# A four-layer network on one Trainium2 core: second expert choices of layer 0 in slots of their own, and layer 1's constant tiles written by POOL

## The chip, the cores and the metric

The kernel runs on one core of a Trainium2 chip. That core has five engines with an instruction queue each: PE (TensorE, matrix products), DVE (VectorE), ACT (ScalarE), POOL (GpSimd) and SP (SyncE, which here only issues DMAs). Each queue runs its instructions in order; semaphores make an instruction wait for another engine or for a DMA. The metric is the device time of one execution in microseconds (us).

## The reference, cut to what matters

Four layers stand one after another. Each takes a layer norm of x (4 sequences of 512 tokens of 128 numbers) and adds an attention part and a feed-forward part to it:

```
xn = layernorm(x)
x = x + L0_attn(xn) + L0_ffn(xn)     # ... the same for L1, L2, L3
```

Layer 0's attention has a window of 64 keys. The feed-forward parts of layers 0 and 1 are mixtures of 8 experts: every token goes to the two experts of highest probability, and the result is the sum of both outputs times their gates.

```
top_w, top_idx = top_k(softmax(h @ router.T), 2)
y = sum over the two: gate * expert(h)
```

## The kernel before

**Stages.** `run` (L1716) traces `setup`, `l0`, `l1_zeros`, `l0_ffn`, `l1_attn`, `l1_ffn`, `l2_attn`, `l3`. A scheduler orders each engine's queue from its own estimate of readiness. Inside a block marked `manual_schedule` the instructions of PE, DVE, ACT and POOL keep the order in which they were written, but instructions from outside the block may be put between them when the scheduler believes them ready.

**Layer 0's attention** (`l0`) loops over 32 half-tiles n (16 tiles of 128 tokens, 8 heads each) and five steps of run-out. One step makes scores (PE, L355 and L361), row maxima (DVE, L372 and L373), exponentials (ACT, L384), then turned weights, weighed values (L411, L413, L414) and projections (L430, L431) of the steps before. Four times in a step, at `pull()`, a piece of other work is put into the queues: up to a generator's next `yield`. That other work is, in order, the layer norms, the small attention of the feed-forward part (`mix`), and `route`.

**Routing** (`route`, L1170) finds for each token its two experts and their ranks by comparing all pairs of 8 probabilities (1024 numbers a partition: L1180, L1183, L1184, L1187, L1191), and a place for each (token, choice) in a list of slots that is sorted by expert. Then it sends rows of tokens to their slots in DRAM by 32 indirect DMAs from POOL (L1250), each of 128 rows: 16 tiles by two choices, all into one tensor `slots`. The framework sees two writes of one tensor as dependent, so each of them waits until the one before has landed.

**The expert stage** (`on_slots`, L664) reads the slots in 10 groups of four tiles: SP loads a group (L679, three buffers), PE turns it (L682), ACT copies it, DVE copies the expert's weights (L650), PE multiplies (L656, L688), DVE copies the result out (L693), SP stores it (L694). POOL gathers the results by the same indices (L1260).

**Constants of layer 1** (`l1_zeros`, L949): six tiles for layer 1's attention (kn, qn0, qn1, vv0 to vv2) are zeroed on DVE (L959), and columns of ones are put in (L963, L964, L967). They lie in a pool at the right end of SBUF, where the pools of layer 0 have been; the first of them waits for what used that memory last, among it `rows`, from which the 32 indirect DMAs read.

`setup` also fills `slots` with zeros (L91), so that rows that no token takes hold numbers.

Of the kernel before, what the change touches and what calls it, by code (L numbers as in the profile page):

```python
# [9 lines left out]
F32 = mybir.dt.float32  # L10
# [3 lines left out]
ALU = mybir.AluOpType  # L14
# [3 lines left out]
P = 128  # L18
B, T, D = 4, 512, 128
# [7 lines left out]
SLOT_TILES = (2 * NTOK + E * (P - 1)) // P  # L27


def bc(ap, axis, n):  # L30

    a = ap.unsqueeze(axis)
    shape = list(a.shape)
    shape[axis] = n
    return a.to_broadcast(shape)


class Net:
# [5 lines left out]
    def setup(self):  # L44
        self.routed, self.sending = {}, False

        self.sides = []
        nc, tc, ctx, io = self.nc, self.tc, self.ctx, self.io
        self.const = const = ctx.enter_context(tc.tile_pool(name="const", bufs=1))
        self.keep = keep = ctx.enter_context(tc.tile_pool(name="keep", bufs=1))  # L50
        self.work = ctx.enter_context(tc.tile_pool(name="work", bufs=2))

        self.x = keep.tile([P, NT, D], F32, tag="x", name="x")
        self.xn = keep.tile([P, NT, D], F32, tag="xn", name="xn")

        self.xnT_wide = keep.tile([P, 64 + NTOK], F32, tag="xnT", name="xnT")
        self.xnT = self.xnT_wide[:, 64:]
        nc.gpsimd.memset(self.xnT_wide[:, 0:64], 0.0)
        xin = io["x"].rearrange("(t p) d -> p t d", p=P)
        for b in range(B):  # L60
            nc.sync.dma_start(self.x[:, b * TPB : (b + 1) * TPB, :], xin[:, b * TPB : (b + 1) * TPB, :])

        self.w = {}

        self.first_stack = ExitStack()
        self.first = self.first_stack.enter_context(tc.tile_pool(name="first", bufs=1))
        self.load("l0_", nc.sync)
        self.load("l0f_", nc.sync)

        self.ident = const.tile([P, P], F32, tag="ident", name="ident")  # L70
        make_identity(nc, self.ident)
        self.identb = const.tile([P, P], BF16, tag="identb", name="identb")
        nc.vector.tensor_copy(self.identb, self.ident)
        self.ones = const.tile([P, P], F32, tag="ones", name="ones")
        nc.gpsimd.memset(self.ones, 1.0)

        with tc.tile_pool(name="masks", bufs=1) as tmp:
            self.masks(tmp)


        self.before = const.tile([P, P], F32, tag="before", name="before")
        nc.gpsimd.affine_select(self.before, self.ones, [[1, P]], ALU.is_gt, 0.0, base=0, channel_multiplier=-1)
        self.tile_no = const.tile([1, SLOT_TILES, E], F32, tag="tile_no", name="tile_no")
        nc.gpsimd.iota(self.tile_no, [[1, SLOT_TILES], [0, E]], base=0, channel_multiplier=0, allow_small_or_imprecise_dtypes=True)

        dram = ctx.enter_context(tc.tile_pool(name="rows", bufs=1, space=bass.MemoryType.DRAM))
        self.slots = dram.tile([SLOT_TILES * P, D], F32, tag="slots", name="slots")
        self.results = dram.tile([SLOT_TILES * P, D], F32, tag="results", name="results")
        empty = const.tile([P, D], F32, tag="empty", name="empty")
        nc.gpsimd.memset(empty, 0.0)  # L90
        nc.sync.dma_start(self.slots.rearrange("(t p) d -> p t d", p=P), bc(empty, 1, SLOT_TILES))  # L91

        self.parts0 = keep.tile([P, TPB, 2, D], F32, tag="parts0", name="parts0")


        self.bd = const.tile([P, P], F32, tag="bd", name="bd")
        nc.gpsimd.affine_select(self.bd, self.ones, [[-8, 16], [0, 8]], ALU.is_ge, 0.0, base=0, channel_multiplier=1)
        nc.gpsimd.affine_select(self.bd, self.bd, [[8, 16], [0, 8]], ALU.is_ge, 0.0, base=7, channel_multiplier=-1)

        self.low = const.tile([P, E, E], F32, tag="low", name="low")  # L100
        nc.gpsimd.affine_select(
            self.low, self.ones[:, 0 : E * E].rearrange("p (e f) -> p e f", f=E), [[1, E], [-1, E]], ALU.is_gt, 0.0,
            base=0, channel_multiplier=0,
        )
# [559 lines left out]
    def on_slots(self, layer, sb, ps1, tokens, hidden, w2):  # L664


        nc = self.nc
        expert = self.routed[layer][2]
        slots = self.slots.rearrange("(t p) d -> p t d", p=P)
        results = self.results.rearrange("(t p) d -> p t d", p=P)  # L670
        GROUP = 4
        for t0 in range(0, SLOT_TILES, GROUP):
            n = min(GROUP, SLOT_TILES - t0)
            _, es = nc.values_load_multi_w_load_instructions(
                expert[0:1, t0 : t0 + n], engines={mybir.EngineType.PE, mybir.EngineType.DVE}, min_val=0, max_val=E - 1,
                skip_runtime_bounds_check_because="a count of experts, at least 0, and no more than 7 by a minimum",
            )
            xs = sb.tile([P, GROUP, D], F32, tag="xs", name="xs")
            nc.sync.dma_start(xs[:, 0:n, :], slots[:, t0 : t0 + n, :])  # L679
            pt = ps1.tile([P, GROUP, P], F32, tag="xs", name="xs_ps")  # L680
            for i in range(n):
                nc.tensor.transpose(pt[:, i, :], xs[:, i, :], self.ident)  # L682
            xT = sb.tile([P, GROUP, P], F32, tag="xT", name="xT")
            tokens(xT[:, 0:n, :], pt[:, 0:n, :])
            y_ps = ps1.tile([P, GROUP, D], F32, tag="y", name="y_ps")
            for i, parts in hidden(xT, es):
                for c, h in enumerate(parts):
                    nc.tensor.matmul(  # L688
                        y_ps[:, i, :], h, w2[:, bass.ds(es[i], 1), c, :].rearrange("p a d -> p (a d)"), start=(c == 0),
                        stop=(c == len(parts) - 1),  # L690
                    )
            y = sb.tile([P, GROUP, D], F32, tag="ys", name="ys")
            nc.vector.tensor_copy(y[:, 0:n, :], y_ps[:, 0:n, :])  # L693
            nc.sync.dma_start(results[:, t0 : t0 + n, :], y[:, 0:n, :])  # L694
# [254 lines left out]
    def l1_zeros(self):  # L949

        nc = self.nc
        self.zero_stack = ExitStack()
        sb = self.zero_stack.enter_context(self.tc.tile_pool(name="z1", bufs=1, side="right"))

        qn = [sb.tile([P, 2, TPB, 16, 32], BF16, tag=f"qn{i}", name=f"qn{i}") for i in range(2)]
        kn = sb.tile([P, 2, TPB, 4, 32], BF16, tag="kn", name="kn")
        vv = [sb.tile([P, 2, TPB, 4, 32], F32, tag=f"vv{i}", name=f"vv{i}") for i in range(3)]
        for t in [kn] + qn + vv:
            nc.vector.memset(t, 0.0)  # L959

        for t in qn:
            for c in range(3):
                nc.vector.memset(t[32 * c : 32 * c + 32, :, :, :, 26 + c : 27 + c], 1.0)  # L963
        nc.vector.memset(kn[:, :, :, :, 24:26], 1.0)  # L964
        for t in vv:
            for hf in range(2):
                nc.vector.memset(t[:, hf, :, :, 16 * hf + 4 : 16 * hf + 5], 1.0)  # L967
        self.l1_tiles = qn, kn, vv

    def l1_attn(self):  # L970
# [199 lines left out]
    def route(self, layer, sb, bank, pr, rows):  # L1170


        nc, keep = self.nc, self.keep
        self.softmax8(sb, pr)
        a = sb.tile([P, NT, E, E], BF16, tag="t2_a", name="t2_a", bufs=1)
        c = sb.tile([P, NT, E, E], BF16, tag="t2_c", name="t2_c", bufs=1)
# [4 lines left out]
        if layer == "l0":  # L1181
            yield
        near.tensor_tensor(a, a, bc(self.low, 1, NT), ALU.mult)  # L1183
        nc.vector.tensor_tensor(c, other, own, ALU.is_gt)  # L1184
        if layer == "l0":
            yield
        near.tensor_tensor(a, a, c, ALU.add)  # L1187
        for _ in range(0 if layer == "l0" else 3):
            yield
        rank = sb.tile([P, NT, E], F32, tag="r_rank", name="r_rank", bufs=1)  # L1190
        nc.vector.tensor_reduce(rank, a, AX.X, ALU.add)  # L1191
        sel = sb.tile([P, NT, E], F32, tag="r_sel", name="r_sel", bufs=1)
        nc.vector.tensor_scalar(sel, rank, 1.5, None, ALU.is_lt)
        yield

        ct = bank()[:, 0 : 2 * NT * E].rearrange("p (k t e) -> p k t e", k=2, t=NT)
        nc.tensor.matmul(ct[:, 0, :, :], self.before, sel, start=True, stop=True)
# [36 lines left out]
        index = keep.tile([P, 2, NT], I32, tag=layer + "r_ix", name="r_ix", bufs=1)  # L1234
# [9 lines left out]
        for tt in range(NT):  # L1244
            for k in range(2):
                if layer == "l0" or tt < 6 or k == 0:
                    yield
                if layer == "l0" and k and tt % 4 == 3:
                    yield
                nc.gpsimd.indirect_dma_start(  # L1250
                    self.slots[:, :], bass.IndirectOffsetOnAxis(ap=index[:, k, tt : tt + 1], axis=0), rows[:, tt, :], None
                )
        self.routed[layer] = index, gate, expert

# [568 lines left out]
```

## Time and profile before

| | |
|---|---|
| median of 9 runs | 1299.41 us (1296.92 to 1305.3) |
| the profiled execution | 1307.66 us, of which the span of its instructions is 1305.8 us |
| PE busy | 1047.2 us, 80% of the span |
| DVE, ACT, POOL busy | 806.8, 730.4 and 446.4 us |
| mean granted PE clock | 0.878 of full speed |
| DMA | 35.35 MB, mean 27 GB/s |

The stages by their first and last instructions in the trace: layer 0's attention from the start to 348.6 us; its expert stage to 401.7 us; layer 1's attention to about 787 us; layer 1's experts to about 892 us; layers 2 and 3 to the end. A duration is printed per instruction, or in total when several alike are merged (x8). In square brackets stands how long the engine sat idle before, and what ended that. A wait is listed as "engine, line <- what it waited for: us in total, times, longest".

### The profile page before, as it was taken

How to read it: one execution, taken by the hardware profiler on the slowest of the kernel's cores; microseconds unless marked ns; L12 is line 12 of the kernel's file. 1: busy time of each engine (PE TensorE's matmuls, PEld its weight loads, DVE VectorE, ACT ScalarE, POOL GpSimd, SP SyncE). 2: the span in 40 equal slices, each digit the busy share in tenths (PEclk: the TensorE clock that was granted, in tenths of full speed). 3: DMA queues.
4: the chain of work that ended last, by engine and by line, in shares of the span. 5: the costliest groups of instructions: out<-in, count | busy, mean ns of one | idle time of the engine just before them, and what ended most of it. 6: DMA issues, size and time to landing. Idle time of an engine off the chain costs nothing.

```text
span 1305.8 us, 27780 instructions
## 1 busy us (share of the span) xinstructions
PE 1047.2 (80%) x11397; PEld 657.1 (50%) x11428; DVE 806.8 (62%) x1842; ACT 730.4 (56%) x1301; POOL 446.4 (34%) x579
## 2 busy tenths in 40 slices
PE   5897897994783587888888877993678988999887
PEld 3575676773682244455544447992323333434254
DVE  5485877762533765888788833553557867767343
ACT  4675675783431246677575662221457767876732
POOL 4554652333002554371333321003371542622200
PEclk9799999997896567989888987996579989999899
DMA  7000000000134200000000001211000000000001
GB/s 232 1 2 1 1 2 2 16 26 28 49 88 145 105 15 4 12 8 3 2 3 26 26 18 51 64 31 35 13 15 3 16 3 1 1 1 1 1 1 33
DMA packets 38891, 35.35 MB, mean 27 GB/s; under 512 B 4653, under 2 KB 35694, under 8 KB 38254
## 3 DMA queue, kind: packets, MB, share of 16 engines
q1 hardware_dynamic: 34670, 25.18, 6.1%
q0 software_dynamic: 4096, 8.40, 2.1%
q8 instruction: 91, 1.49, 0.4%
q14 instruction: 34, 0.28, 0.1%
HBM read 20.65 MB, written 12.91 MB: 26 GB/s over the span
## 4 chain that ended last, share of the span: by engine, by line
PE 32%; DVE 14%; ACT 10%; POOL 6%; issue 4%; DMA 1%; another core or an unknown queue 0%; ACTq 0%; POOLq 0%; DVEq 0%
PE o_ps L827 5%; ACT p L818 5%; PE sq_ps L748 5%; DVE max L782 5%; PE gu L1333 4%; DVE negm L786 3%; PE y_ps L688 2%; PE sk_ps L748 2%; PE qs_ps L802 1%; PE po L942 1%; POOL xn L206 1%; PE po L1671 1%; PE tr L232 1%; POOL parts L1260 1%; PE piece L1435 1%
## 5 line engine op out<-in xcount | busy, mean ns | idle before, releaser
L818 ACT ACTIVATE p<-sk_ps 128x1024 f32<-128x1024 f32 x288 | 279.9, 1028 | 103.4 <-PE sk_ps L748 48.4
L782 DVE TENSOR_REDUCE max<-sq_ps 128x4 f32<-128x512 f32 x320 | 203.9, 685 | 68.3 <-PE sq_ps L748 39.7
L786 DVE TENSOR_REDUCE negm<-sq_ps 128x1 f32<-128x512 f32 x256 | 163.4, 684 | 67.6 <-PE sq_ps L748 65.3
L748 PE MATMUL sq_ps<-kb,qb 64*128 64x512 bf16 (+3 forms) x640 | 138.1, 348 | 43.2 <-DVE negm L786 13.4
L827 PE MATMUL o_ps<-p,vv 128*32 128x128 f32 (+3 forms) x2304 | 171.4, 416 | 1.1 <-issue 0.7
L748 PEld LDWEIGHTS <-qb 32*128 32x128 bf16 (+1 forms) x1152 | 50.4, 96 | 170.9 <-issue 151.7
L1260 POOL DMA_INDIRECT parts<-results,r_ix x64 | 63.4, 991 | 199.2 <-DMA results<-ys 103.1
L384 ACT ACTIVATE p<-s_ps,nm,rs 128x128 f32<-128x128 f32 x256 | 93.2, 485 | 27.3 <-DVE nm L373 27.3
L827 PEld LDWEIGHTS o_ps<-p,vv 128*32 128x32 f32 x2304 | 61.3, 116 | 72.0 <-issue 63.9
L748 PE MATMUL sk_ps<-qs,kb 64*128 64x512 bf16 (+3 forms) x640 | 74.4, 340 | 10.3 <-ACT p L818 8.9
L804 ACT COPY qs<-qs_ps 128x1024 bf16<-128x1024 bf16 x32 | 32.4, 1012 | 65.4 <-PE qs_ps L802 65.4
L1333 PE MATMUL gu<-xT,gu 128*128 128x128 f32 x468 | 60.3, 284 | 1.5 <-ACT xT L1320 1.5
L1333 PEld LDWEIGHTS gu<-xT,gu 128*128 128x128 f32 x468 | 57.2, 199 | 2.1 <-ACT xT L1320 2.1
L372 DVE TENSOR_REDUCE nm<-s_ps 128x4 f32<-128x512 f32 x64 | 41.3, 684 | 23.7 <-PE s_ps L361 23.6
L1335 ACT ACTIVATE silu<-gu 128x384 f32<-128x384 f32 x39 | 19.1, 491 | 62.5 <-PE gu L1333 62.5
L361 PEld LDWEIGHTS s_ps<-kT,qT 64*64 64x64 f32 x1024 | 30.5, 143 | 41.2 <-issue 41.2
L1250 POOL DMA_INDIRECT slots<-rows,r_ix x32 | 31.2, 976 | 53.3 <-DMA slots<-rows,r_ix 52.4
L748 PE MATMUL sq_ps<-kd,qb 32*128 32x128 bf16 x512 | 35.8, 233 | 16.8 <-DVE max L782 14.8
L1250 POOL DMA_INDIRECT slots<-xn,r_ix x32 | 30.9, 965 | 53.6 <-DMA slots<-xn,r_ix 52.8
L324 POOL TENSOR_TENSOR sq<-q 128x1024 f32<-128x1024 f32 x12 | 22.8, 1904 | 61.6 <-ACT q L319 61.6
L1327 DVE COPY gu<-w_l1f_gu 128x704 f32 x39 | 20.4, 527 | 37.7 <-PE gu L1333 37.7
L232 PE MATMUL piece<-ident,xn 128*128 128x128 f32 x32 | 8.7, 371 | 41.2 <-DVE xn L206 39.6
(437 smaller groups left out, 2252.3 us busy)
## 6 DMA issues: line engine op xcount, KB each, us to landing
xs<-slots SPq DMA_DIRECT2D x18, 256.0 KB
results<-ys SPq DMA_DIRECT2D x18, 256.0 KB
w_l1f_gu<-in_l1f_gu SPq DMA_DIRECT2D x1, 2816.0 KB
slots<-empty SPq DMA_DIRECT2D x1, 2496.0 KB
w_l0f_w<-in_l0f_w SPq DMA_DIRECT2D x2, 1024.0 KB
w_l1f_down<-in_l1f_down SPq DMA_DIRECT2D x1, 1536.0 KB
x<-in_x SPq DMA_DIRECT2D x4, 256.0 KB
parts<-results,r_ix POOLq DMA_INDIRECT x64
```

The lines of the kernel that those rows point to most:

```text
L361: nc.tensor.matmul(ss[a][cols, k, :], qT[rows, 4 * u + k, cols], kT[rows, u, c0 : c0 + P], start=False, stop=(k == 3))
L372: nc.vector.tensor_reduce(nm[:, a, :], ss[a], AX.X, ALU.max, negate=True)
L384: nc.scalar.activation(p[:, a, k, :], ss[a][:, k, :], AF.Exp, bias=nm[:, a, k : k + 1], scale=rs[:, h : h + 1])
L748: nc.tensor.matmul(s[:, c : c + w], lhs(rows, which(hf, r), slice(i * P, i * P + P)), rhs(rows, which(hf, r), slice(o0, o0 + w)), start=(x ...
L782: nc.vector.tensor_reduce(places[step](maxima[n % 2][:, r, :, :]), s.rearrange("p (x c) -> p x c", c=P), AX.X, ALU.max)
L786: nc.vector.tensor_reduce(m[:, r, step : step + 1], s, AX.X, ALU.max, negate=True)
L804: nc.scalar.copy(qs, pt.rearrange("p x i c -> p x (i c)"))
L818: nc.scalar.activation(p, ks[pr], AF.Exp, scale=scale)
L827: nc.tensor.matmul(o[32 * r : 32 * r + 32, q0 : q0 + w], states[b]["v"](hf, j, g, r), p[r // 2][:, r % 2, c : c + w], start=(step == 0 and ...
L1250: nc.gpsimd.indirect_dma_start(self.slots[:, :], bass.IndirectOffsetOnAxis(ap=index[:, k, tt : tt + 1], axis=0), rows[:, tt, :], None)
L1260: self.nc.gpsimd.indirect_dma_start(parts[:, i, k, :], None, self.results[:, :], bass.IndirectOffsetOnAxis(ap=index[:, k, b * TPB + i : b ...
L1333: nc.tensor.matmul(gu[:, k, c, :], wgu[:, k, c * P : (c + 1) * P], xT[:, i, :], start=True, stop=True)
```

## The change

Three things are changed.

First, layer 0's second choices go to a DRAM tensor `slots2` of their own, also filled with zeros at the start. The two indirect DMAs of a tile no longer write the same tensor. The expert stage of layer 0 loads both tensors and DVE adds them (128 partitions by 512 numbers a group). Layer 1 goes on using `slots` alone.

Second, the memsets of `l1_zeros` are issued on POOL in place of DVE.

Third, the yields of `route` are moved in layer 0: the comparisons come one to a pull, three pulls more stand before the first indirect DMA, and the four additional pulls among the indirect DMAs are gone.

```
+        self.slots2 = dram.tile([SLOT_TILES * P, D], F32, tag="slots2", name="slots2")
...
-        nc.sync.dma_start(self.slots.rearrange("(t p) d -> p t d", p=P), bc(empty, 1, SLOT_TILES))
+        for t in (self.slots, self.slots2):
+            nc.sync.dma_start(t.rearrange("(t p) d -> p t d", p=P), bc(empty, 1, SLOT_TILES))
...
             nc.sync.dma_start(xs[:, 0:n, :], slots[:, t0 : t0 + n, :])
+            if layer == "l0":
+                xs2 = sb.tile([P, GROUP, D], F32, tag="xs2", name="xs2")
+                nc.sync.dma_start(xs2[:, 0:n, :], self.slots2.rearrange("(t p) d -> p t d", p=P)[:, t0 : t0 + n, :])
+                nc.vector.tensor_tensor(xs[:, 0:n, :], xs[:, 0:n, :], xs2[:, 0:n, :], ALU.add)
...
         for t in [kn] + qn + vv:
-            nc.vector.memset(t, 0.0)
+            nc.gpsimd.memset(t, 0.0)
...
-                nc.vector.memset(t[32 * c : 32 * c + 32, :, :, :, 26 + c : 27 + c], 1.0)
-        nc.vector.memset(kn[:, :, :, :, 24:26], 1.0)
+                nc.gpsimd.memset(t[32 * c : 32 * c + 32, :, :, :, 26 + c : 27 + c], 1.0)
+        nc.gpsimd.memset(kn[:, :, :, :, 24:26], 1.0)
...
-                nc.vector.memset(t[:, hf, :, :, 16 * hf + 4 : 16 * hf + 5], 1.0)
+                nc.gpsimd.memset(t[:, hf, :, :, 16 * hf + 4 : 16 * hf + 5], 1.0)
...
         near.tensor_tensor(a, a, bc(self.low, 1, NT), ALU.mult)
+        if layer == "l0":
+            yield
         nc.vector.tensor_tensor(c, other, own, ALU.is_gt)
...
-        for _ in range(0 if layer == "l0" else 3):
+        for _ in range(1 if layer == "l0" else 3):
             yield
...
-        yield
+        for _ in range(2 if layer == "l0" else 1):
+            yield
...
-                if layer == "l0" and k and tt % 4 == 3:
-                    yield
+                slots = self.slots2 if layer == "l0" and k else self.slots
                 nc.gpsimd.indirect_dma_start(
-                    self.slots[:, :], bass.IndirectOffsetOnAxis(ap=index[:, k, tt : tt + 1], axis=0), rows[:, tt, :], None
+                    slots[:, :], bass.IndirectOffsetOnAxis(ap=index[:, k, tt : tt + 1], axis=0), rows[:, tt, :], None
```

## The prediction

> **What bounds the kernel now.** The busy shares (PE 80%, DVE 62%) come first, but they are means over stages. The chain that ended last doesn't help here: the pieces that it lists begin at 412.9 us, and the change lies before that. So I read the waits between 300 and 349 us, the end of layer 0's attention, where the page's 40 slices show a dip:
>
> ```profile
> ACT p L384 <- DVE nm L373: 22.9, 2, 21.0
> PE s_ps L355 <- ACT p L384: 21.1, 1, 21.1
> DVE kn L959 <- DMA slots<-rows,r_ix: 20.6, 1, 20.6
> ```
>
> These are one wait seen three times. PE waits for ACT, ACT for DVE's small multiply L373, and L373 stands behind L959, the memset of kn, which waits for the indirect DMAs. VectorE's timeline shows the order of that queue:
>
> ```profile
> 304.77 1.41 DVE L372 TENSOR_REDUCE nm<-s_ps 128x4 f32<-128x512 f32 x2 [1.35 <-PE s_ps L361]
> 326.74 0.48 DVE L959 MEMSET kn<- 128x512 uint32 x1 [20.56 <-DMA slots<-rows,r_ix]
> 327.14 0.10 DVE L373 TENSOR_TENSOR nm<-nm,rs 128x8 f32<-128x8 f32 x1
> ```
>
> The memset was put between the last maxima but one and their scaling. The indirect DMAs run late: the 32 first issue at 241.6 us, the last at 324.2 us, one per 2.5 us, because each waits for the one before:
>
> ```profile
> L1250 POOL DMA_INDIRECT slots<-rows,r_ix x32 | 31.2, 976 | 53.3 <-DMA slots<-rows,r_ix 52.4
> ```
>
> Next the stretches (us; then busy PE, PEld, DVE, ACT, POOL; then granted clock, DMA share, GB/s):
>
> ```profile
> 255.00:298.00 43.00, 42.69 (x565) 33.05 (x570) 28.09 (x69) 37.18 (x103) 15.64 (x16) 1.00 0.08 25
> 305.00:327.00 22.00, 2.69 (x46) 2.38 (x46) 1.42 (x3) 0.58 (x1) 7.76 (x9) 0.64 0.08 28
> 327.00:335.00 8.00, 6.16 (x73) 4.97 (x72) 7.09 (x13) 3.96 (x10) 0.00 (x0) 0.50 0.00 0
> 349.00:402.00 53.00, 44.76 (x351) 41.85 (x351) 16.50 (x49) 21.31 (x32) 0.00 (x0) 0.97 0.32 94
> ```
>
> The undisturbed loop is bound by PE (42.69 of 43 us), 7.2 us a step (maxima at 254.84, 269.27, 283.67, 298.09, two steps apart); DVE has about 2.4 us a step free. After the stall the granted clock is 0.50 for 8 us. The expert stage is PE's too; DVE is busy for a third of it.
>
> **The stall and the run-out.** Idle gone: 20.6 us. Then I rebuild the run-out without memsets and with a warm clock. L373 comes at 306.2, where L372 ends. The exponentials of ACT (2.90) end at 309.2; the last scores start about 0.4 us before that, as the ones at 303.15 did, and take 0.65 + 1.10 us (1.10 at full clock, 1.99 after the stall); maxima 1.3, so the last exponentials start at 312.1 in place of 335.8: 23.7 us earlier. From there to the last DVE instruction of the stage the trace takes 12.8 us, with two memsets of vv and all the small ones between DVE's other work. With the durations of the rows (exponentials 2.9, turns 1.1, copies 0.7, weighing 1.15, DVE 1.2 under PE's projection 2.05, turns 1.1, copies 0.7, projection 2.05: 11.75 and a little for hand-overs) I get about 11.9, so 0.9 less. Sum: **−24.6 us**. Ends: −20.6 (the wait alone) to −28 (memset time, 8.1 us, all on the path).
>
> **What is late next.** The indirect DMAs must not be. Two of one tile now write different tensors, so only every second waits. POOL's rate without waits is that of the gathers, which read one tensor and don't depend on each other:
>
> ```profile
> 405.33 0.98 POOL L1260 DMA_INDIRECT parts<-results,r_ix  x1 [80.12 <-DMA w_l_lam<-in_l_lam]
> 406.62 0.95 POOL L1260 DMA_INDIRECT parts<-results,r_ix  x1 [0.31 <-issue]
> ```
>
> 1.26 us each, so a pair fits the 2.5 us of one landing, and 32 take 40 us. Three pulls more move the first from 241.6 to about 244 us; the last lands near 287, far before the run-out ends (about 322). If nothing overlaps, they take 82 us and end at 327.
>
> **Memsets on POOL.** They wait for the last landings, then run from about 287. POOL has nothing else until its gather (idle for 80.1 us before 405.33), so they cost nothing while they end before that. Time on POOL: vv 128x1024 f32 at 0.92 each (half of L1308's 1.80), kn and qn about 0.5 to 0.9 and 1.8 to 3.4 each (L1049 on POOL is listed as bf16, 315 ns for 256 numbers, L1387 214 ns for 128), and 13 small ones under 0.22: 9 to 13 us in all. Could they slow DVE, which is in the loop's slack then? One row says that the two engines can block each other:
>
> ```profile
> 238.74 1.97 POOL L324 TENSOR_TENSOR sq<-q 128x1024 f32<-128x1024 f32 x1 [23.99 <-ACT q L319]
> 239.31 1.54 DVE L1232 SCALAR_TENSOR_TENSOR r_sel<-r_rank,pr 128x128 f32<-128x128 f32 x1
> ```
>
> L1232 takes 0.28 elsewhere. Bounds: 0 to +13 us if every memset stopped DVE; I take 0, because DVE's rows in that stretch read PSUM (L372, L397, L414) and a memset reads nothing, unlike L324.
>
> [...]
>
> **Route, one pass a pull.** In steps 19 to 22 the maxima start at 214.24, 230.40, 242.27, 246.88, then 254.84: 40.6 us against 4 x 7.2, so 11.8 us over. In step 19 DVE has 4.8 us of its own and 10.7 of route (short waits within it counted), in step 20 4.8 and 7.4. Moved, about 6.1 of route (softmax 1.8, passes 1.23, 1.21, 1.22, 0.68) stay in step 19, about 6 come in step 20, 4.7 in step 21. DVE's excess over 7.2 a step falls from 8.3 + 5.0 to 3.7 + 3.6 + 2.3, so by 3.7 of 13.3. As the old order gives part of its excess back (step 21 took 4.6 us), I take **−2.5 us** (0 to −4).
>
> **The expert stage.** Added: 10 loads, 10 adds on DVE. SBUF adds of f32 in the trace: 128 numbers 0.29, 320 0.49, 640 0.83; so 512 take 0.69, in all 6.8 us. In the steady part the loads are there long before (issue at 372.66 and 373.67, turned at 382.0 and 392.4), and DVE is free for two thirds: 0. The start is different, since nothing can be loaded before layer 0's pools are free:
>
> ```profile
> SPq L679 <- DVE yT L424: 335.5, 1, 335.5
> ```
>
> SP issues at 348.41; PE turns the first group at 351.11 and the second at 352.53, having waited for DMAs both times. Both come before PE's first product in its queue, and so does now the fourth load, not the second. A load of 256 KB takes 0.83 us of all DMA engines (queue q1: 25.18 MB in 6.1% of the span) up to the 1.4 us seen between those two turns. Two loads more are 1.7 to 2.8, the add 0.7, a late third or fourth group up to 1: **+3 us** (1 to 7).
>
> **The second fill of zeros.** 2496 KB more at the start, issued last at 11.2 us; SP's next load is at 348.4 us. 8 us of DMA, 0 us (0 to 1).
>
> **Sum.** −24.6 − 2.5 + 3 = −24.1 us. The profiled execution (1307.66, span 1305.8) would become 1283.6. It stands 8 us above the median of the runs; the terms are absolute waits, so I take them from the median: 1299.41 − 24.1 = **1275.3 us**.
>
> **Rivals.**
> - The indirect DMAs still land one by one (a queue in order). They end at about 244 + 82.5 + 2 = 328, and the expert stage starts some 6 us later than forecast: 1281. For it: nothing in the trace has two indirect writes in flight. Against it: the gathers do overlap. Chance 0.12.
> - POOL's memsets stop DVE: up to 13 us given back, 1288. For it the 1.54 us row, against it what DVE reads there, and its slack. Chance 0.05.
> - More is won: all of the memset time (−28) and the route's −4, the start +1: 1268. For it: the first products run at clock 0.50 until 335 and some half-microsecond hand-overs went with the memsets. Chance 0.13.
> - Slower: DVE's queue is in order, and an add stands ahead of weight copies (L650) of the group that PE works on. If the scheduler puts the adds so early that each waits for its load, each of ten groups pays issue to landing (2.7), the second issue (0.4) and the add (0.7): 38 us against the 27.1 won, so 1310. It decides from 2.7 us a group on. Against it: three buffers, and loads in the trace that land 8 us ahead. Chance 0.04.
> - The change doesn't do what it says: another instruction that waits for the indirect DMAs or for the loads is put into DVE's queue before the run-out, and the stall stays: 1299 to 1302. Against it: the loads can't be issued before the run-out has ended, and adds that depend on them can't be thought ready earlier. Chance 0.04.
>
> **How the numbers follow.** The forecast has 0.62. Its own bounds (−28 to −20.6, route 0 to −4, start 1 to 7, runs of before spread over 8 us) give about 1268 to 1282. With the neighbours, 1267 to 1284 leaves less than 2 in 10 out. Faster by over 0.3% (what a measurement of this kernel can tell from no change, 3.9 us): 0.62 + 0.12 + 0.05 + 0.13 = 0.92, plus 0.01 of the slower cases' luck: 0.93; within 0.3%: 0.03; slower: 0.04.
>
> **What the next profile would show.** Right: no wait of L373 or ACT over 3 us near 306; L1250 at about 1.26 us, the last before 290; the last L431 near 322; L959 on POOL between 285 and 305; maxima of steps 19 to 21 about 10 to 11 us apart; first L682 about 5 us after the first L679. Wrong: L1250 waiting 1.5 us each time, a DVE add that waits for DMA xs2 in every group, or DVE rows that double beside POOL's memsets. A granted clock that stays at 0.50 for longer in layer 1 (it did between 436 and 476 us with PE busy) would move the time by some microseconds either way, without any of these steps.

## The result and the profile after

The change made the kernel **slower**, by 0.8%: 1313.91 us median (1309.22 to 1319.83, 20 runs) against 1303.09 (62 runs of before beside them), a ratio of 1.0084 [1.0069, 1.0098]. The forecast was 1275.3 us, with a range of 1267 to 1284. The profiled execution took 1310.29 us (span 1308.5, mean granted clock 0.882).

First the views that answer to those of before. The stall in the run-out is gone: VectorE's timeline at the same two maxima (step n = 30; L375 and L376 are L372 and L373 of before) shows 0.46 us of waiting where 20.56 stood.

```profile
339.08 1.29 DVE L375 TENSOR_REDUCE nm<-s_ps 128x4 f32<-128x512 f32 x2 [1.17 <-PE s_ps L364]
340.83 0.17 DVE L376 TENSOR_TENSOR nm<-nm,rs 128x8 f32<-128x8 f32 x1 [0.46 <-ACT pT L398]
```

But these maxima start at 339.08 us, and those of before at 304.77. The waits between 245 and 292 us show the place (waited for: us in total, times, longest; "remote" is a releaser that the profile can't name):

```profile
ACT qT L345 <- remote: 28.9, 2, 20.5
PEld o_ps L414 <- ACT qT L345: 25.5, 2, 17.4
PE o_ps L414 <- ACT qT L345: 24.9, 2, 16.9
DVE pT L400 <- remote: 21.6, 1, 21.6
DVE nm L375 <- remote: 14.1, 2, 12.0
```

No wait of that size stood there before: the longest between 245 and 292 us was 3.4 us, POOL's for the DMA before. The stretches (us; then busy PE, PEld, DVE, ACT, POOL; then granted clock, DMA share, GB/s):

```profile
256.00:264.00 8.00, 0.80 (x3) 0.37 (x2) 0.39 (x1) 0.00 (x0) 6.08 (x7) 0.50 0.15 49
264.00:272.00 8.00, 0.00 (x0) 0.00 (x0) 2.46 (x5) 0.00 (x0) 5.96 (x7) 0.50 0.15 49
272.00:280.00 8.00, 1.14 (x16) 0.94 (x16) 0.00 (x0) 0.69 (x1) 6.17 (x7) 0.50 0.17 57
280.00:288.00 8.00, 1.12 (x7) 0.69 (x7) 0.00 (x0) 0.69 (x1) 5.38 (x7) 0.50 0.12 41
```

PE, DVE and ACT stand nearly still for 32 us, and only POOL works. What it does is the 32 indirect DMAs of layer 0 (L1259, L1250 of before), and they run just as the prediction wanted, with almost no wait for a landing (1.2 us in all, of 18.9 us of idle time):

```profile
L1259 POOL DMA_INDIRECT slots<-rows,r_ix x32 | 31.0, 969 | 18.9 <-DVE r_ix L1245 9.3 <-issue 8.3 <-DMA slots<-rows,r_ix 1.2
```

They issue from 244.87 to 284.46 us, one every 1.26 us. Three timelines tell what the others wait for. PE turns the queries into pt_q and goes on to other matrices behind them in its queue:

```profile
251.62 0.66 PE L343 MATMUL pt_q<-ident,q 128*128 128x128 f32 x4 [0.39 <-ACT sq L325]
...
256.47 0.80 PE L396 MATMUL pt_p<-ident,p 128*128 128x128 f32 x3 [0.83 <-issue]
274.22 1.14 PE L414 MATMUL o_ps<-v,pT 128*64 128x65 f32 x16 [16.95 <-ACT qT L345]
...
287.46 0.27 PE L414 MATMUL o_ps<-v,pT 128*64 128x65 f32 x1 [3.23 <-issue]
289.56 0.27 PE L414 MATMUL o_ps<-v,pT 128*64 128x65 f32 x1 [1.84 <-issue]
```

ACT, which has only to copy that pt_q, wakes at 273.48, and DVE, which copies pt_p, at 290.31:

```profile
273.48 0.69 ACT L345 ACTIVATE qT<-pt_q,w_l_qkw 128x512 f32<-128x512 f32 x1 [20.46 <-remote]
```

```profile
290.31 0.69 DVE L400 COPY pT<-pt_p 128x512 f32<-128x512 f32 x1 [21.64 <-remote]
```

PE's timeline has pt_q's matrices at 251.62 and 252.59 us, ahead of L396's, the last of which began at 256.47: the word of them took 17 us or more to reach ACT. In the other direction there is no delay: ACT's copy ends at 274.17 and PE's L414 starts at 274.22. PE's own issue is slow as well: single matrices come 2 to 3 us apart at 287 to 290 us, where 32 of L414 take 1.15 us elsewhere. From 290.3 us on, 5 us after the last indirect DMA left POOL, all is as it was. **What is held up is PE: its signals to the others and its own issue.** DVE's and ACT's instructions take as long as ever: 0.69 us each for L400 and L345, as L397 and L342 took before (medians 0.68 and 0.69).

The sum of the parts, by first instructions in both traces: the maxima of step 18 start 1.2 us later, at 205.49 us; route gives back 2.3 up to step 22; steps 22 to 30 cost 35.4 (57.9 before, 93.3 after), which is the standstill; the run-out gives back 25.2 (from the maxima of step 30 to the first load of the expert stage 43.6 before, 18.4 after); the expert stage costs 2.2 (from its first load to its last store 53.7, then 55.9). Together +11.3; the medians differ by 10.8. The two profiled executions differ by only 2.6, because all that follows layer 0's experts took 8.7 us less in the one after. That the second fill of zeros causes the first 1.2 us is not shown: over all profiled executions the maxima of step 18 start between 201.5 and 207.2 us with that fill and between 203.9 and 204.4 without it (before, e1, e17).

### The profile page after: what moved, and what is told of

It is laid out like the page before. It is cut to its first block, busy times and chain, and to the rows that moved or that the text cites. A ratio compares the mean times of both kernels' runs of the same rounds, so it can differ in the third digit from the quotient of the medians.

```text
span 1308.5 us, 27820 instructions
## 1 busy us (share of the span) xinstructions
PE 1042.5 (80%) x11397; PEld 653.0 (50%) x11428; DVE 805.5 (62%) x1833; ACT 731.8 (56%) x1301; POOL 461.9 (35%) x598
## 3 DMA queue, kind: packets, MB, share of 16 engines
q0 software_dynamic: 4096, 8.40, 2.1%
## 4 chain that ended last, share of the span: by engine, by line
PE 44%; DVE 21%; ACT 12%; POOL 11%; issue 6%; another core or an unknown queue 3%; DMA 2%; SPq 1%; ACTq 0%; DVEq 0%; POOLq 0%
DVE max L789 6%; PE o_ps L834 5%; PE sq_ps L755 5%; ACT p L825 5%; PE gu L1342 4%; PE y_ps L695 4%; DVE negm L793 3%; PE sk_ps L755 2%; POOL xn L209 2%; PE up L659 1%; PE z L433 1%; PE s_ps L364 1%; PE qs_ps L809 1%; PE po L1680 1%
## 5 line engine op out<-in xcount | busy, mean ns | idle before, releaser
L755 PE MATMUL sq_ps<-kb,qb 64*128 64x512 bf16 (+3 forms) x640 | 137.5, 344 | 43.6 <-DVE negm L793 12.9
L375 DVE TENSOR_REDUCE nm<-s_ps 128x4 f32<-128x512 f32 x64 | 41.2, 684 | 37.1 <-PE s_ps L364 23.0
L414 PE MATMUL o_ps<-v,pT 128*64 128x65 f32 x1024 | 39.0, 228 | 30.5 <-ACT qT L345 24.9
L414 PEld LDWEIGHTS o_ps<-v,pT 128*64 128x64 f32 x1024 | 33.8, 140 | 37.5 <-ACT qT L345 26.7
L1259 POOL DMA_INDIRECT slots<-xn,r_ix x32 | 30.9, 965 | 55.6 <-DMA slots<-xn,r_ix 52.5
L345 ACT ACTIVATE qT<-pt_q,w_l_qkw 128x512 f32<-128x512 f32 x32 | 20.6, 695 | 45.8 <-remote 28.9
```

What stands on the lines that cost most here:

```text
L375: nc.vector.tensor_reduce(nm[:, a, :], ss[a], AX.X, ALU.max, negate=True)
L414: nc.tensor.matmul(o[cols, k, :], pT[:, a, k, cols], v[:, 1 - blk, 2 * u + a, :], start=True, stop=True)
L755: nc.tensor.matmul(s[:, c : c + w], lhs(rows, which(hf, r), slice(i * P, i * P + P)), rhs(rows, which(hf, r), slice(o0, o0 + w)), start=(x ...
```

## The experiments

**The theory (A):** a run of indirect DMAs from POOL with no gap holds up PE. **Rivals:** the memsets on POOL (B); two writes in flight at a time (C); the traffic itself, in bytes or rows (D). A common measure: from the maxima of step 22 to those of step 30, an undisturbed loop takes 56.6 us (e2, e5 and e16 agree to 0.01 us). The change takes 93.3. e3, e4, e6 to e8, e10 and e12 to e15 are single executions: their times have no interval, and the steps in their traces carry the argument. In the edits, line numbers shift by a few lines: the indirect DMAs are L1259 or L1260. The runs lie on four chips: A (e1 to e4), B (e5 to e8), C (e9 to e12), D (e13 to e17).

**e1, one chain again.** The second tensor is taken out; the memsets and route stay as changed.

```
-                slots = self.slots2 if layer == "l0" and k else self.slots
+                slots = self.slots
```

> The changed kernel with one slots tensor again (no second fill, no second load, no add): the indirect DMAs wait for one another, 2.5 us each; memsets on POOL and the moved yields stay. Theory A (indirect DMAs issued back to back, every 1.26 us, hold up PE and its signals): the standstill of 251 to 290 us is gone, steps stay at 7.2 us, the last DMA lands near 244 + 82.5 + 2 = 328, the expert stage starts there; 18 to 24 us faster than before. Theory B (the memsets on POOL do it): the standstill stays, no faster than the changed kernel.

1279.16 us, ratio 0.9824 [0.9779, 0.9869]. The DMAs come 2.5 us apart, steps 22 to 30 take 57.1 us, and there is no standstill. The price is at the end: the run-out is done first and the first turn of the expert stage waits 13.4 us for the last landing and its load.

**e2, spaced.** Both tensors, and POOL fills a pad of 768 numbers between any two indirect DMAs.

```
+            self.pad = mb.tile([P, 768], F32, tag="pad", name="pad")
...
                 nc.gpsimd.indirect_dma_start(...)
+                if layer == "l0":
+                    nc.gpsimd.memset(self.pad, 0.0)
```

> The changed kernel with a memset of 768 numbers on POOL (some 0.75 us, into a tile that nothing reads) after each indirect DMA of layer 0, so that they start every 2.0 us. Theory A, as a matter of the rate: no standstill, or a short one; last DMA near 245 + 64 = 309 us, run-out ends near 322; some 20 to 26 us faster than before. Theory C (two indirect writes in flight at the same time are enough, whatever the rate; a landing takes 2.5 us, so they still overlap): the standstill lasts as long as the DMAs do, 60 us or more; slower than the changed kernel by 20 us.

1273.43 us, ratio 0.9811 [0.9775, 0.9847]: no standstill, steps 22 to 30 in 56.6 us. POOL's timeline:

```profile
246.15 0.98 POOL L1260 DMA_INDIRECT slots<-rows,r_ix  x1 [0.17 <-issue]
247.12 0.76 POOL L1264 MEMSET pad<- 128x768 f32 x1
248.04 0.97 POOL L1260 DMA_INDIRECT slots<-rows,r_ix  x1 [0.17 <-issue]
```

POOL waits for "issue" and not for a landing: at 1.89 us apart and 2.5 us to land (the distance of the chained ones in e1), two are still in flight at a time. C falls: 0.6 us more between two of them is enough.

**e3, memsets back on VectorE.**

```
-            nc.gpsimd.memset(t, 0.0)
+            nc.vector.memset(t, 0.0)
```

> The changed kernel with layer 1's memsets on DVE again. Theory A: the standstill stays as it is (some 35 us lost between 246 and 296 us); the memsets find the DMAs landed, so DVE doesn't wait for them; within 6 us of the changed kernel. Theory B (the memsets on POOL hold DVE up): the standstill goes, 30 us faster than the changed kernel.

1312.46 us, and the standstill stays (maxima of steps 22 and 24 at 242.58 and 292.99), with PE's own issue in front of the waits. B falls as its cause.

```profile
PEld o_ps L414 <- issue: 17.6, 9, 4.0
PE o_ps L414 <- issue: 17.0, 10, 3.8
```

**e4, direct DMAs.** The 32 indirect DMAs become direct ones from the same queue, with the same bytes, in token order (tokens do not reach their experts' slots).

```
+                    nc.gpsimd.dma_start(slots[tt * P : tt * P + P, :], rows[:, tt, :])
```

> The changed kernel, but each of layer 0's 32 indirect DMAs from POOL is a direct DMA from POOL of the same 64 KB to rows in the order of tokens (the rows don't reach their experts' slots, so layer 0's expert part is left wrong, and all that follows has other numbers). If the row by row addressing is what holds PE up: no standstill, 30 us or more faster than the changed kernel. If any dense stream of DMAs that POOL issues does it: a standstill between 250 and 290 us as in the changed kernel.

1267.33 us. All 32 go out within 17.3 us, 0.54 us apart, and PE's steps beside and behind them are undisturbed (maxima at 232.86, 241.93, 247.71, 255.09 in steps 21 to 24):

```profile
230.01 17.26 POOL L1260 DMA_DIRECT2D slots<-rows  x32
```

More than twice the rate of DMAs and bytes does no harm, so D falls for bytes: only the indirect ones show the standstill. Two things differ besides: these DMAs don't wait for the index and so start 15 us earlier, and they write consecutive rows. Whether the indirect instruction or the scattered addresses matter is not separated by any run.

**e5 to e8, on the second chip.** Four kernels, to find the limiting rate, whether the delay builds up, and whether direction or rows matter: a pad of 384 numbers (e5); four memsets behind every fourth DMA (e6); reads in place of the writes (e7); 64 rows a DMA (e8).

```
+                        rows[:, (tt + 8 * k) % NT, :], None, self.slots[:, :],       # e7
...
+                    slots[:, :], bass.IndirectOffsetOnAxis(ap=index[0:h, k, tt : tt + 1], axis=0), rows[0:h, tt, :], None   # e8: h = 64
```

> The change with a memset of 384 numbers behind each of layer 0's 32 indirect DMAs in place of 768, so that they come about 1.5 us apart in place of 1.89. If what holds PE up is a rate that something can only just not serve at 1.26 us (threshold near 1.3), the standstill is gone and the time is that of the 768 one or 1 to 3 us less, 1270 to 1275. If the limit lies near 1.8, PE loses a part: steps between 250 and 300 us take 8 to 12 us in place of 7.3 and the time is 1280 to 1305.

> The same number of memsets of 768 numbers, but four in a row behind each fourth indirect DMA: bursts of four at 1.26 us, then a pause of about 3 us; the mean rate is that of the spaced one. If the delay of PE builds up over several indirect DMAs (in the change the loop still ran for about 6 us after the first), the pauses let it go and the time is 1270 to 1278. If every two that follow each other at 1.26 us cost PE by themselves, half or more of the 35 us comes back: 1290 to 1305.

> The change with its 32 indirect writes of layer 0 turned into 32 indirect reads at the same place and rate (rows of slots gathered into the tile of rows; no token reaches its slot, so layer 0's experts work on zeros). If it is the issue of indirect DMAs by POOL that holds PE up, in whichever direction, the standstill of 30 to 40 us between 250 and 290 us stays and the time is 1300 to 1315. If it is the writes to DRAM at scattered places, it goes and the time is 1265 to 1275.

> The change with each of the 32 indirect DMAs sending 64 rows in place of 128 (the other half of the rows is left out). If PE is held up by the number of rows (descriptors) per us, and POOL still needs about 1 to 1.26 us for each, the standstill goes and the time is 1265 to 1275. If it is the number of indirect instructions per us, it stays: 1300 to 1315. If POOL needs only half as long for half the rows, the rate of rows stays and the standstill is half as long: 1280 to 1295.

e5: 1263.22 us, ratio 0.9818 [0.9774, 0.9862]; e6: 1252.14; e7: 1280.74; e8: 1275.15 (before on this chip: 1288.67). None of the four has the standstill, not even e7 and e8, whose DMAs come every 1.25 and 1.20 us. On these four alone I would have put it down to 128-row writes. But the change itself was not among them, so I ran it and e7's reads on other chips before I believed it.

e7 and e8 have another pause after their DMAs, of 8 and 11 us (steps 22 to 30 in 64.7 and 67.3): rival B in small. VectorE's timeline of e7, then POOL's:

```profile
289.49 8.43 DVE L304 TENSOR_SCALAR rsk<-rsk 128x4 f32<-128x4 f32 x1
289.57 8.35 DVE L400 COPY pT<-pt_p 128x512 f32<-128x512 f32 x1
290.55 7.37 DVE L416 RECIPROCAL ri<-o_ps 128x4 f32<-128x4 f32 x1
```

```profile
287.66 6.97 POOL L966 MEMSET qn<- 128x4096 bf16 x2
294.56 2.75 POOL L966 MEMSET vv<- 128x1024 f32 x3
```

L304, a tiny operation from SBUF to SBUF whose median is 0.17 us in this trace, is stuck until the large memsets are over (they end at 297.31 us, L304 at 297.92), and the queue behind it with it. In e8 it is 10.31 us (memsets to 296.63, L304 to 297.23).

**e9 to e12, on a third chip.** The change once more; e7's reads with the memsets on VectorE; the bursts with an interval; a pad of 192 numbers.

> The change itself once more, as the measure for the runs beside it, since the runs e5 to e8 were made on another chip than e1 to e4. If the standstill belongs to the kernel, PE's steps stop for 30 to 36 us between 245 and 295 us here too and the ratio to the kernel before is 1.005 to 1.012. If it depends on the chip, e7 and e8 say nothing yet, and the time here may be 20 to 35 us lower.

> The 32 indirect reads of e7 (no token reaches its slot) with layer 1's memsets back on VectorE. If reads at 1.25 us do not hold PE up, the steps between 245 and 290 us take 6 to 8 us again, as in e7, beside a standstill in the change itself on the same chip. If e7's pause from 287.6 to 303.4 us came from VectorE's instruction L304, which lasted 8.4 us while POOL's memsets ran, that pause is gone too, and the time stands 25 to 45 us under that of the change. If the pause came from the end of the indirect DMAs, it stays.

> The bursts of four of e6 with an interval. Against the kernel before on the same chip: ratio 0.970 to 0.980 if e6's one time was typical, 0.980 to 0.985 if it was luck and the kernel is as good as the evenly spaced ones.

> A memset of 192 numbers behind each indirect DMA, so about 1.3 to 1.4 us from one to the next. If the limit lies between 1.26 and 1.3 us, there is no standstill and the time is that of e5 within 8 us. If PE is held up in proportion to the rate, 5 to 20 us of the standstill come back. If it is the two chains of writes that run without a gap, in which each finds its predecessor but one just landed, the standstill goes as soon as POOL waits for nothing else: no standstill either, but POOL's rows show waits for landings in the change and none here.

e9: 1310.1 us, ratio 1.0081 [1.0051, 1.0110], steps 22 to 30 in 94.1 us: the standstill is here. e10: 1316.98, and reads have it as well (96.4 us), so my guess of the reads fell; whether e7's pause goes with VectorE's memsets could not be seen beside it. e11: 1276.81, ratio 0.9851 [0.9814, 0.9888], steps 22 to 30 in 64.4 us, so bursts of four already cost 8 us. e12, 1.41 us apart: 1295.45 and 77.8 us. Its stretches show PE losing part of its time (the columns are those of the stretches above):

```profile
252.00:258.00 6.00, 3.28 (x37) 2.63 (x37) 3.55 (x6) 3.19 (x7) 5.34 (x9) 0.79 0.13 44
258.00:264.00 6.00, 5.08 (x21) 3.29 (x19) 0.60 (x2) 2.37 (x8) 5.29 (x10) 0.50 0.13 44
```

The loss falls with the distance between two DMAs: 37 us at 1.26 (e9), 21 at 1.41 (e12), 0 at 1.89 (e2, e16). (The 1.56 us of e5 were tried on chip B alone.)

**e13 to e16, on a fourth chip.** The change, and the same kernels as e7, e8 and e2, side by side.

> The change itself, as the measure for e14 to e16. Standstill of 30 to 36 us between 245 and 295 us if this chip is of the kind of the first and third, none (steps of 6 to 9 us, time about 30 us under the others) if it is of the kind of the second.

> The same kernel as e7 (reads in place of the writes; no token reaches its slot). If the chip decides, it does what e13 does: a standstill of 30 us or more wherever e13 has one, and none where e13 has none. If the engine of layer 1's memsets decides, it has none even where e13 has one, as in e7.

> The same kernel as e8 (64 of each 128 rows are left out). Where e13 has a standstill: if indirect instructions per us count, it is as long here, since they come every 1.2 us; if rows per us count, PE loses less than 10 us between 245 and 285 us. Where e13 has none, this says nothing.

> The kernel of e2, indirect DMAs 1.89 us apart. Ratio to the kernel before 0.978 to 0.985 on any chip if that spacing is enough everywhere; above 0.985 if some chips lose PE time at this rate too.

e13: 1303.43 us, steps 22 to 30 in 93.1 us. e14: 1304.55 and 93.6. e15: 1309.51 and 95.0. e16: 1273.84, ratio 0.9828 [0.9747, 0.9910], and 56.6. So chip B is the exception: the same two kernels have the standstill on D and not on B. One stretch of e8 on B, and the same stretch of e15 on D:

```profile
264.00:270.00 6.00, 5.95 (x84) 5.33 (x89) 4.67 (x11) 5.96 (x16) 3.90 (x5) 1.00 0.11 27
```

```profile
264.00:270.00 6.00, 0.00 (x0) 0.00 (x0) 0.01 (x1) 0.00 (x0) 4.47 (x6) 0.50 0.11 27
```

The same DMAs move the same 27 GB/s; PE is busy for 5.95 of 6 us on the one and not at all on the other. And e15 settles rows against instructions: half the rows, half the bytes, one DMA per 1.20 us, and as long a standstill. D falls for rows too. On chips A, C and D, what counts is how closely indirect DMAs follow each other on POOL (1.20 to 1.26 us: standstill; 1.89 us: none), whatever their direction (C, D), rows or bytes (D).

**e17, the memsets alone.** The kernel before with layer 1's memsets on POOL, and nothing else.

> The kernel before with layer 1's memsets on POOL and nothing else: one chain of indirect DMAs 2.5 us apart, no second tensor, route as before. The wait of 20.6 us in VectorE's queue must go; the run-out then ends near 325 us and the expert stage waits only for the last landing at about 327, so its first turn comes near 331 in place of 351: 18 to 22 us less than before, ratio 0.983 to 0.987. If e1's gain came from route and the pulls that were taken out, it is under 10 us.

1269.1 us against 1287.05, ratio 0.9862 [0.9804, 0.9919]. (Beside e13 to e16 the kernel before took 1297.61 on this chip; so ratios are compared, each with the runs beside it.) The last maxima but one come at 303.99 us as before, no stall follows, and the first turn of the expert stage comes at 330.25 (before: 351.11). This turn still waits 8.0 us for its load, which SP issues at 327.50, when the last of the 32 (issued at 325.06) has landed:

```profile
PE xs_ps L682 <- DMA xs<-slots: 8.0, 1, 8.0
```

So most of what e1, e2 and e16 win (ratios 0.981 to 0.983) comes from four lines that change engine. What the second tensor and route add lies within the intervals. Here, too, VectorE pays a little for POOL's memsets: four weight copies (L650) last 4.17 us at 334.37, where six last 1.44 at 323.18; POOL's memsets of vv end at 338.38 us, and these copies at 338.54.

## Why the prediction was wrong

**The step that failed is "What is late next".** It said: "POOL's rate without waits is that of the gathers", 1.26 us, so that 32 take 40 us, and it charged nothing to the other engines. The rate was right to the digit (244.87 to 284.46 us), and the last landed at about 286.8, before 290 as forecast. The rate itself was the price: 35.4 us on PE, in place of 0. My only worry there was that the DMAs would come too slowly. The kernel before had them 2.5 us apart, and its gathers came 1.25 us apart in runs of eight; its trace held no run of indirect DMAs without a gap that was longer than eight. I bounded the rate by the nearest row, and did not bound what that rate does to an engine that has nothing to do with POOL.

The other steps held:

- Stall and run-out: −24.6 forecast, −25.2 measured.
- Route, one pass a pull: −2.5 forecast, −2.3 measured; the maxima of steps 19 to 22 start at 215.44, 226.07, 236.71 and 245.77 us, 9 to 11 us apart.
- Expert stage: +3 forecast, +2.2 measured; first turn 4.5 us after the first load, forecast about 5.
- Second fill of zeros: 0 (0 to 1) forecast; no delay that stands out from the spread of the runs.
- Without the standstill the sum is what e2 (1273.43 us) and e16 (1273.84) show: 1275.3 was the time of a kernel with the indirect DMAs spaced.

**Memsets on POOL: right for the wrong reason.** They ran from 286.83 to 301.9 us, at the place forecast but for 15.1 us in place of 9 to 13, and cost nothing there. I had argued that DVE's rows in that stretch read PSUM and that a memset reads nothing; that this decides was an estimate of mine, which no trace of before shows. For such rows it held: L400 at 290.31 us took its 0.69 us beside the memset of qn. But not all rows of DVE are of that kind. L304 reads and writes SBUF, and e7 and e8 show it stuck for 8.4 and 10.3 us. It was held for longer than one memset (3.5 us at most): until the whole close row of large memsets was over. What sets L304 apart is not shown: L302, which also reads and writes SBUF, took its 0.42 us at 289.03 us in e7, beside the memset of qn. I had not looked for a row that does not read PSUM. In the change, L304 came only at 297.62 us, after the large memsets had ended, and took 0.37: that was luck.

**Of the rivals**, none was this one. Landing one by one was tested in effect by e1 and would have been the better outcome (1279.16 us). The slower case that I priced (1310), adds that wait for their loads in each of ten groups, came about in small: six times an add waited, 8.5 us in all, but the expert stage grew by 2.2 us only.

```profile
DVE xs L686 <- DMA xs<-slots: 8.5, 6, 2.4
```

That its 1310 lies near the measured 1313.91 is chance; the time was lost elsewhere.

**What stays open.** Why indirect DMAs in a close row delay PE's signals and issue, and why chip B does not show it (each kernel ran there once or in one set of runs, and the change itself not at all, so it could also be the chip's condition at that time). The runs exclude bytes, rows, direction, two in flight and the memsets; they don't show the path. That PE's instructions were loaded late is unlikely, if queue q8 ("instruction") is what loads them (91 packets in the change, one for 251 of PE's 22,825 matrix products and weight loads): in the change's trace, 224 instructions of PE lie between the two loads of q8 around the standstill, at 245.4 and 293.7 us, where 190 to 337 lie between two loads in a row elsewhere; and PE is back at its pace at 290.3 us, before the second of them. Spacing the DMAs is what helped here (e2 and e16: 56.6 us for steps 22 to 30 at 1.89 us apart).

## What to carry to other kernels

When a change takes away a wait between DMAs that POOL issues, price not only POOL's rate but what the other engines do beside it: look for "remote" and "issue" waits on PE in a trace that has such a row of DMAs. Indirect DMAs that don't bound the kernel may as well be spaced by other work of POOL or left in one chain: 2.5 us apart in one chain gave the same time within the intervals as two chains 1.89 us apart (ratios 0.9824 in e1, 0.9811 in e2). And split a change into its parts before it is judged: here one part won some 18 us by itself and another lost 35.

## What the runs showed of the hardware

- On three of four chips, 32 indirect DMAs from POOL 1.20 to 1.26 us apart held up PE: steps 22 to 30 took 93.1 to 96.4 us (the change, e9, e10, e13 to e15) in place of 56.6, and in e3 the maxima of steps 22 and 24 lay 50.4 us apart. In the change PE was busy for 3.06 us of the 32 from 256 to 288 us, and was back at its pace 5 us after the last DMA. At 1.41 us apart the loop lost 21 us in 46 (e12), in bursts of four 8 us in 63 (e11), at 1.89 us nothing (e2, e16). On the fourth chip, 1.25 and 1.20 us apart, there was no standstill (e7, e8). Direct DMAs from POOL 0.54 us apart did no harm (e4: maxima of steps 21 to 24 5.8 to 9.1 us apart).
- A standstill is seen in the granted clock, too: in the change it is 0.50 in every stretch from 256 us, 11 us after the first indirect DMA, to 288 us.
- POOL takes 3.5 us to zero 128 x 4096 numbers of bf16 (L966 of the change, 6.97 for two), VectorE 1.77 (L966 of e10, written there as half as many uint32).
